# Order of sums and products at the seams of a two-layer kernel with Strassen products

## The chip, the cores and the metric

The kernel runs on one core of a Trainium2 chip. The core has a matrix engine (TensorE, PE in the profile), three engines for elementwise work (VectorE or DVE, ScalarE or ACT, GpSimd or POOL), a queue engine for transfers (SyncE or SP), and 16 DMA engines between device memory (DRAM) and the on-chip memories SBUF and PSUM. Each engine runs its own list of instructions in order, and waits on semaphores where it needs what another made. The metric is device microseconds of one execution; the time of a kernel is the median of its runs.

## The reference

There are eight batches of 256 tokens with 1024 features, in float32. Two layers follow each other, each with a residual:

```
layer 0:  y   = x + x·W0ᵀ + b0 + c_b · (x·(2·mask_b − 1))     mask_b: 8 integer matrices of 1024 x 1024
layer 1:  out = y + y·W1ᵀ + b1 + 2 · (y·A_s)·B_s               A_s, B_s: adapters of rank 16, s = itok[b]
```

So layer 0 has one weight matrix per batch, and layer 1 has one for all, with a small adapter per batch.

## The kernel before

Everything is computed transposed: weights are the stationary operand, tokens the moving one.

**Layer 0.** For each batch an effective weight is built in 8 pieces of 128x1024. ScalarE turns the integer mask into (2c·mask − c) (L237), VectorE adds the piece of W0ᵀ (L245), to which the identity was added so that the residual is in the product. `load` (L173) issues the transfers of a piece on SP; `build` does the two steps. The constant `BY_HALF` (L19) gives the number of first pieces, of batch 0, that are loaded and built as two halves, so that the product can begin with half a piece. Batch 0 (`first_batch`, matmuls L303) takes the pieces as they come. Batches 1 and 2 (`first_layer`, L278) are plain products. Batches 3 to 7 (`SEVEN`, L20; `class Seven`) use the Winograd form of Strassen's algorithm: seven products of half size (matmuls L419, into the PSUM tiles X, Y and Z) from sums of weight blocks (s1 to s4, `weight_sum`, L356) and of token blocks (t1 to t4, `token_sum`, L373). `Seven.operands` (L375) is a generator that gives these builds and sums in order; `Sevens.begin` (L500) makes some of them early, during other work, and `Sevens.run_one` keeps ten steps ahead of the products. Operands after the first `FREE_OPERANDS` (L491) of a group are ordered behind the end of the second layer of the group before. Results are read by ScalarE (`with_bias`, L438) and VectorE (`add`, L445).

**Layer 1.** `second_layer` (L694) is run for two groups of four batches, group 0 after batch 3 and group 1 after batch 7. Four batches are treated as a matrix of blocks, and Strassen's form is used twice: seven outer products named A11, A12, S1, S2, S4, S3, A22 (runs 0 to 6), each of them made of seven inner ones in X, Y and Z (`product`, L711, matmuls L718, four per inner product, two passes each in float32). The weight sums, the leaves, are made by VectorE during layer 0, stored to DRAM by POOL (`keep`, L533), and loaded by SP (`load_leaves`, L703, L708). Sums of y for an outer operand are made by `outer_sum` (L874, the T tiles) and its four inner sums by `Right.sums` (L685 to L691). The S3 weights are made again from reloaded blocks: `again` (L615) loads the tiles A11 and A21, L607 subtracts, `inner_in_place` (L596) makes the sums in place.

`run` (L785) is one outer product. Its accumulator X goes on being added to: it is read (`read`: a ScalarE copy, L772, where nothing is to be added, else a VectorE add, L774), then the next product is added into the same bank, and the following read takes the difference into account. So a product into X waits for the read before it. In run 0, `down` (L748) makes the adapters' first product: 64 matmuls passes into psh (L753), then four ScalarE activations into h_sb (L762). `up` (L727) makes the second, into banks G (L736), copied by ScalarE (L746). Quarters of the output are combined on VectorE (`add`, L860) and stored by POOL for group 0 (L781).

**What sets the order.** Instructions are recorded in the order of the text, but a scheduler may place them otherwise where it estimates that an operand is late. `behind(what)` (L144) fixes that an instruction is placed after the latest one remembered under that name. `ordered` (L891) does this for the sums of y. Generators given to `run` as `beside` are advanced by one step at fixed places, and emptied at the end of the run.

At the start `idle` (L98) issues matmuls on a zero tile, so that TensorE is busy while the first transfers come; h_sb, zeroed by VectorE (L95), serves as that tile and later holds the adapters' first product.

Of the kernel before, what the change touches and what calls it, by code (L numbers as in the profile page):

```python
# [9 lines left out]
F32 = mybir.dt.float32  # L10
# [4 lines left out]
P = 128  # L15
OH = 512
CG = 2
OQ = 256
BY_HALF = 3  # L19
SEVEN = (3, 4, 5, 6, 7)  # L20
SCALING = 2.0

# [2 lines left out]
def kernel(  # L25
# [38 lines left out]
    nc = tc.nc  # L64
    B, NG, _, _, T = xT.shape
# [25 lines left out]
    one_row = const.tile([1, P], F32, tag="one_row", name="one_row")  # L91
    nc.vector.memset(one_row, 1.0)

    h_sb = const.tile([P, T], F32, tag="h", name="h_sb")
    nc.vector.memset(h_sb, 0.0)  # L95
    idle_ps = psum.tile([P, T], F32, tag="ps", name="idle_ps")

    def idle(n: int):  # L98
        for _ in range(n):
            nc.tensor.matmul(idle_ps, lhsT=h_sb[:, :P], rhs=h_sb, start=True, stop=True)  # L100

    idle(1)
    c_ps = psum.tile([P, B], F32, tag="ps", name="c_ps")
    spread = nc.tensor.matmul(c_ps, lhsT=one_row, rhs=c_row, start=True, stop=True)
    with tc.issue_after(spread.ins):
# [38 lines left out]
    def behind(what: str):  # L144
        return tc.issue_after(anchors[what].ins) if what in anchors else nullcontext()
# [183 lines left out]
    class Seven:  # L329
# [45 lines left out]
        def operands(self):  # L375

            add, sub = nc.vector.tensor_add, nc.vector.tensor_sub
            for j in range(2):
                for a in range(2):
                    self.block(0, j, a)  # L380
                    yield
            self.token_sum("t1")
            yield
            self.token_sum("t2")
            yield
            for a in range(2):
                self.block(1, 1, a)
                yield
                self.block(1, 0, a)
                yield  # L390
                self.weight_sum("s1", add, "a21", "a22", a)
                yield
                self.weight_sum("s2", sub, "s1", "a11", a)
                yield
            self.token_sum("t3")
            yield
            for a in range(2):
                self.weight_sum("s3", sub, "a11", "a21", a)
                yield
            for a in range(2):  # L400
                self.weight_sum("s4", sub, "a12", "s2", a)
                yield
            self.token_sum("t4")
            yield
# [39 lines left out]
        def add(self, i, v, ps):  # L444
            anchors["weights"] = nc.vector.tensor_add(self.out(i, v), ps, self.out(i, v))  # L445
            if i == v:
                anchors["adds"] = anchors["weights"]
# [39 lines left out]
        HALVES = 14  # L487

    OPERANDS_AHEAD = 10
    FREE_OPERANDS = 7  # L490

    class Sevens:

# [12 lines left out]
        def run(self, y, between):  # L506

            for i, batch in enumerate(self.batches):
                batch.y = y[batch.b % GB]
                between(batch.b)  # L510
                self.run_one(i, batch)
# [182 lines left out]
    def second_layer(group: int, y, first, first_steps, second):  # L694
# [3 lines left out]
        a = la_of[group]  # L698
        halves = [[[y[2 * j + v][i] for v in range(2)] for j in range(2)] for i in range(2)]
        (b11, b12), (b21, b22) = halves  # L700
        left_leaf, right = {}, {}
# [9 lines left out]
        def product(ps, l, r, first=False, by_tile=False):  # L711
            order = [(c, j) for c in range(CG) for j in range(2)]
            if by_tile:
                order.sort(key=lambda cj: cj[1])

            with behind("products") if first else nullcontext(), behind("adapters"):
                for c, j in order:
                    anchors["inner"] = nc.tensor.matmul(  # L718
                        ps[:, j, :],
                        lhsT=l[:, c, j * P : (j + 1) * P],  # L720
                        rhs=r[:, c, :],
                        start=first and c == 0 and j == 0,
                        stop=False,
                        skip_group_check=True,
                    )
# [59 lines left out]
        def run(n, name, r, seed, out, dest=None, beside=None, early=None, mid=None, late=None, then=None):  # L785

            leaf = {k: left_leaf.pop((name, k)) for k in ("a11", "s1", "s2", "a12", "s3", "a22", "s4")}
            other = seed or {uv: None for uv in UV}  # L790
            beside = beside or iter(())
            X = banks.pop(n)

            def done(uv):
                if dest:
                    store(out[uv], *dest, *uv)
                if then:
                    then(uv)

            read(out[0, 0], X, other[0, 0])  # L800
            Z = bank(f"Z_{group}_{n}")
            product(Z, leaf["s1"], r.t["t1"], first=True)
            if early:
                early()
            product(X, leaf["s2"], r.t["t2"])
            next(beside, None)
            read(out[0, 1], X, other[0, 1])
            Y = bank(f"Y_{group}_{n}")
            product(Y, leaf["a12"], r.b[1, 0], first=True)
            read(out[0, 0], Y, out[0, 0])  # L810
            done((0, 0))
            if mid:
                mid()
            if n + 1 == len(plan):
                finish(X, Z, leaf, r, other, out, dest, beside, done)
                return
            product(X, leaf["s3"], r.t["t3"])
            next(beside, None)
            read(out[1, 1], X, other[1, 1])
            read(out[1, 1], Z, out[1, 1])  # L820
            done((1, 1))
            load_leaves(plan[n + 1])
            begin(n + 1, plan[n + 1], right[plan[n + 1]])
            next(beside, None)
            product(X, leaf["a22"], r.t["t4"])
            read(out[1, 0], X, other[1, 0])
            done((1, 0))
            next(beside, None)
            if late:
                late()  # L830
            product(Z, leaf["s4"], r.b[1, 1])
            read(out[0, 1], Z, out[0, 1])
            done((0, 1))
            for _ in beside:
                pass
# [19 lines left out]
        def quads(name):  # L855
            two = [pair(f"{name}{u}_{group}") for u in range(2)]
            return {(u, v): two[u][:, v] for u, v in UV}

        def add(o, x):
            nc.vector.tensor_add(o, o, x)  # L860
# [3 lines left out]
        big_t = {}  # L864

        def outer_sum(n, x, y, name):


            big_t[n] = [
                tpool.tile([P, TPH, T], F32, tag="T", name=f"T{n}_{group}_{v}") for v in range(2)  # L870
            ]
            right[name] = Right(f"T{n}_{group}", big_t[n])
            for v in range(2):
                nc.vector.tensor_sub(big_t[n][v], x[v], y[v])  # L874
                yield
            yield from right[name].sums()
# [7 lines left out]
        def next_weights(n):  # L884
            if group + 1 < NGROUP:
                while sevens[group + 1].made < n:
                    sevens[group + 1].begin(sevens[group + 1].made + 1)
                    yield


        def ordered(steps):  # L891

            while True:
                with behind("reads" if "reads" in own else "layer"):
                    if next(steps, True):
                        return
                yield

        own = {}
        s3 = ordered(later["S3"] if group == 0 else iter(()))  # L900
# [2 lines left out]
        begin(0, "A11", first)  # L903
        for _ in ordered(first_steps):
            pass
        t1 = ordered(outer_sum(1, b12, b11, "S1"))
        e1, c11, c12 = quads("e1"), quads("c11"), quads("c12")
        lower = (c11, c12)
        run(
            0, "A11", first, None, e1,  # L910
            beside=chain(islice(s3, 1), ordered(second.sums()), islice(s3, 4), islice(t1, 2)),
            early=down,
            mid=lambda: up(0, 0, lower),
            late=lambda: up(0, 1, lower),
            then=lambda uv: add(c11[0, 0], e1[0, 0]) if uv == (1, 1) else None,
        )
        for uv in UV[1:]:
            add(c11[uv], e1[uv])
        t2 = ordered(outer_sum(2, b22, big_t[1], "S2"))
        run(  # L920
            1, "A12", second, c11, c11,
# [16 lines left out]
        run(  # L938
            4, "S4", right["S4"], c12, c12,
            dest=(0, 1),  # L940
            beside=ordered(outer_sum(4, b21, big_t[2], "A22")),
            mid=lambda: up(1, 0, upper),
            late=lambda: up(1, 1, upper),
        )
# [1 line left out]
        def add_e5():  # L946

            for uv in UV:
                with behind("reads"):
                    add(c22[uv], e5[uv])  # L950
                yield

        run(5, "S3", right["S3"], e1, e1, beside=chain(add_e5(), next_weights(2)), then=lambda uv: add(c21[uv], e1[uv]))


        next_masks(6)
# [1 line left out]
        def last_quarter():  # L958
            for u, v in UV:
                add(c22[u, v], e1[u, v])  # L960
                store(c22[u, v], 1, 1, u, v)
                yield
# [1 line left out]
        run(  # L964
            6, "A22", right["A22"], c21, c21,
            dest=(1, 0),
            beside=chain(last_quarter(), next_weights(4)),
        )
        nonlocal limit
        limit = n_pieces  # L970


    load_to(LOADS_AHEAD)
# [141 lines left out]
```

## Time and profile before

| what | value |
|---|---|
| time, median of 3 runs | 412.66 us (411.93 to 412.89) |
| the profiled execution | 411.92 us |
| its span in the profile | 410.25 us (the page rounds to 410.3) |
| TensorE busy | 401.6 us, 98% of the span |
| VectorE busy | 312.2 us, 76% |
| ScalarE busy | 136.3 us, 33% |
| granted TensorE clock | 1.00 in every stage |
| layer 0, batches 0 to 2 | 5.7 to 90 us |
| batch 3 by seven products | 90 to 115 us |
| second layer, group 0 | 115 to 211 us |
| batches 4 to 7 by seven products | 211 to 313 us |
| second layer, group 1 | 313 to 407 us |

The span is what the profiler saw of the execution; the execution's time is 1.7 us longer. A line of the page or of the timeline names the engine, the line of the kernel, the operation, the tiles written and read, and in brackets how long the engine stood idle before it and what released it. In a line of the waits stand the engine, its line and tile, what it waited for, and then us in total, times, and the longest. A tile `T_t` stands for the four inner sums of a T tile, `b_t` for those of b11 or b21, `l_S_a<-leaf_S_a` for the load of a leaf.

### The profile page before, as it was taken

The page shows a single profiled execution, that of the slowest core. Times are in us where ns is not written, and L with a number is a line of the kernel's source. Part 1 is how long each engine was busy: PE and PEld are TensorE (multiplying, and loading weights), DVE is VectorE, ACT ScalarE, POOL GpSimd, SP SyncE. Part 2 cuts the span into 40 slices and gives each one's busy share as a digit, 9 for nine tenths or more (in the row PEclk, how much of TensorE's full clock was granted, in tenths as well). Part 3 has the DMA queues.
Part 4 walks back from the last instruction along what each step waited for, and adds up shares of the span by engine and source line. Part 5 has one row for each costly group of instructions (what it writes and reads, how often), then busy time and mean ns, then how long its engine had stood idle before and what let it go on. Part 6 is the DMA issues. An engine that isn't in the chain of part 4 may idle for free.

```text
span 410.3 us, 6785 instructions
## 1 busy us (share of the span) xinstructions
PE 401.6 (98%) x2554; PEld 358.1 (87%) x2554; DVE 312.2 (76%) x446; ACT 136.3 (33%) x221; POOL 52.0 (13%) x102
## 2 busy tenths in 40 slices
PE   8999999999999999999999999999999999999996
PEld 6788888899977887788899999999998788888885
DVE  2447696999834979885999999999922277898593
ACT  4444525782124203132140936538221420102200
POOL 0000152007850131011040000300000000000000
PEclk9999999999999999999999999999999999999999
DMA  7999999980898699676898848732022247655654
GB/s 277 403 403 397 400 410 419 403 321 16 302 350 312 214 309 330 194 254 210 286 378 312 309 162 279 260 95 79 27 63 75 80 129 237 171 153 165 214 154 153
DMA packets 41252, 99.56 MB, mean 243 GB/s; under 512 B 5636, under 2 KB 6148, under 8 KB 41220
## 3 DMA queue, kind: packets, MB, share of 16 engines
q1 hardware_dynamic: 32546, 76.04, 54.3%
q0 software_dynamic: 6224, 18.90, 12.3%
q10 hardware_dynamic: 2450, 4.20, 2.8%
q8 instruction: 20, 0.33, 0.3%
q14 instruction: 12, 0.10, 0.1%
HBM read 79.19 MB, written 19.92 MB: 242 GB/s over the span
## 4 chain that ended last, share of the span: by engine, by line
PE 90%; DMA 4%; DVE 3%; issue 1%; SPq 1%; ACT 0%; DVEq 0%
PE X L718 24%; PE X L419 17%; PE ps L278 13%; PE Z L718 11%; PE Z L419 8%; PE Y L718 5%; PE ps L303 4%; PE Y L419 3%; PE G L736 2%; PE psh L753 2%; DMA w_sb<-w0T 2%; DVE w L245 1%; DMA w<-mask 1%; DMA l_S_a<-leaf_S_a 1%; SPq L197 1%
## 5 line engine op out<-in xcount | busy, mean ns | idle before, releaser
L237 ACT ACTIVATE w<-w,neg_c,two_c 128x1024 f32<-128x1024 int32 (+1 forms) x67 | 78.5, 1207 | 64.1 <-DMA w<-mask 54.5
L245 DVE TENSOR_TENSOR w<-w,w_sb 128x1024 f32<-128x1024 f32 (+1 forms) x67 | 77.3, 1171 | 26.0 <-ACT w L237 16.1
L278 PE MATMUL ps<-x,w 128*128 128x256 f32 x256 | 55.4, 379 | 0.0
L278 PEld LDWEIGHTS ps<-x,w 128*128 128x128 f32 x256 | 48.6, 190 | 6.6
L438 ACT ACTIVATE y<-X,b_sb 128x128 f32<-128x128 f32 x60 | 17.1, 368 | 71.3 <-PE X L419 71.3
L860 DVE TENSOR_TENSOR c<-c,e 128x512 f32<-128x512 f32 x48 | 31.9, 682 | 4.6 <-ACT c L746 4.6
L419 PE MATMUL X<-t,s 128*128 128x128 f32 x288 | 34.0, 276 | 0.6 <-ACT y L438 0.3
L419 PEld LDWEIGHTS X<-t,s 128*128 128x128 f32 x288 | 33.0, 192 | 0.9 <-ACT y L438 0.5
L746 ACT COPY c<-G 128x512 f32<-128x512 f32 x32 | 16.4, 600 | 38.4 <-PE G L736 38.4
L303 PE MATMUL ps<-x,w 128*128 128x256 f32 x128 | 28.2, 381 | 0.9 <-DVE w L245 0.9
L303 PEld LDWEIGHTS ps<-x,w 128*128 128x128 f32 x128 | 24.2, 191 | 4.8 <-DVE w L245 1.5
L772 ACT COPY e<-X 128x512 f32<-128x512 f32 x16 | 9.4, 589 | 49.4 <-PE X L718 46.5
L774 DVE TENSOR_TENSOR e<-Y,e 128x512 f32<-128x512 f32 x8 | 5.5, 689 | 25.8 <-PE Y L718 14.0
L774 DVE TENSOR_TENSOR c<-X,c 128x512 f32<-128x512 f32 (+1 forms) x26 | 16.6, 645 | 8.1 <-PE X L718 7.9
L718 PE MATMUL X<-T_t,l_S_s 128*128 128x256 f32 x96 | 22.7, 379 | 0.0
L419 PE MATMUL X<-t,w 128*128 128x128 f32 x192 | 22.5, 276 | 0.0
L419 PEld LDWEIGHTS X<-t,w 128*128 128x128 f32 x192 | 21.9, 192 | 0.2 <-DVE y L445 0.2
L356 DVE TENSOR_TENSOR s<-w,w 128x1024 f32<-128x1024 f32 x18 | 21.7, 1217 | 0.1
L718 PEld LDWEIGHTS X<-T_t,l_S_s 128*128 128x128 f32 x96 | 18.2, 190 | 2.5
L419 PE MATMUL Z<-t,s 128*128 128x128 f32 x160 | 19.1, 275 | 0.3 <-DVE s L356 0.3
L419 PE MATMUL X<-x,w 128*128 128x128 f32 x160 | 18.8, 275 | 0.0
L419 PEld LDWEIGHTS Z<-t,s 128*128 128x128 f32 x160 | 18.4, 192 | 0.5 <-PE Y L419 0.5
(145 smaller groups left out, 670.7 us busy)
## 6 DMA issues: line engine op xcount, KB each, us to landing
w<-mask SPq DMA_DIRECT2D x61, 512.0 KB, 7.1
l_S_s<-leaf_S_s SPq DMA_DIRECT2D x32, 256.0 KB, 2.9
x<-xT SPq DMA_DIRECT2D x31, 256.0 KB, 7.4
l_A_s<-leaf_A_s SPq DMA_DIRECT2D x24, 256.0 KB, 2.8
l_S_a<-leaf_S_a SPq DMA_DIRECT2D x24, 256.0 KB, 2.8
w<-w1T SPq DMA_DIRECT2D x16, 256.0 KB, 6.9
outT<-c POOLq DMA_DIRECT2D x15, 256.0 KB, 4.6
outT<-c ACTq DMA_DIRECT2D x15, 256.0 KB, 2.5
```

The costliest lines, as they stand in the source:

```text
L237: nc.scalar.activation(w[:, i], m[:, i], AF.Identity, bias=neg_c[:, b : b + 1], scale=two_c[:, b : b + 1],)
L245: weff_at[k] = nc.vector.tensor_add(w[:, i], w[:, i], w0_of(k)[:, i])
L278: nc.tensor.matmul(ps[j // 2][:, j % 2, :], lhsT=w[:, c, j * P : (j + 1) * P], rhs=x_sb[b, g][:, c, :],  start=first and j % 2 == 0, stop= ...
L303: nc.tensor.matmul(ps[ot // 2][:, ot % 2, :], lhsT=w[:, h, j * P : (j + 1) * P], rhs=x_sb[0, c // CG][:, c % CG, :], start=c == 0 and ot % ...
L356: anchors["weights"] = op(s, self.w[x, a], self.w[y, a])
L419: anchors["products"] = nc.tensor.matmul(ps[:, j, :], lhsT=w[:, c, j * P : (j + 1) * P], rhs=r, start=first and a == 0 and c == 0 and j == ...
L438: sent = nc.scalar.activation(self.out(i, v)[:, j, :], ps[:, j, :], AF.Identity, bias=b0_sb[:, ot : ot + 1])
L718: anchors["inner"] = nc.tensor.matmul(ps[:, j, :], lhsT=l[:, c, j * P : (j + 1) * P], rhs=r[:, c, :], start=first and c == 0 and j == 0, s ...
L746: nc.scalar.copy(dest[b // 2][u, b % 2], ps[b])
L772: anchors["copies"] = nc.scalar.copy(out, ps)
L774: own["reads"] = anchors["reads"] = nc.vector.tensor_add(out, ps, other)
L860: nc.vector.tensor_add(o, o, x)
```

## The change

1. `BY_HALF` goes from 3 to 4: the fourth piece of batch 0, too, is loaded and built by halves.
2. The idle matmuls read a constant zero tile and not h_sb, so that h_sb isn't zeroed by VectorE at the start; two of them stand first and not one.
3. In `Seven.operands`, t1 and t2 come after the first two blocks of the lower row and not before them. This holds for batches 3 to 7.
4. `FREE_OPERANDS` goes from 7 to 6.
5. `product`: the first product into a bank was placed behind layer 0's last product alone; it is now placed behind the latest product of the second layer also. Together with the accumulation into one bank this puts TensorE's products in the order of the text.
6. `second_layer`: the first step of S3, the four sums of b21 (`second.sums`) and the two T1 tiles, which were advanced within run 0, are made ahead of run 0. The three adds into c11 after it are placed behind the latest read.
7. The weights of the next group's first batch: two pieces are built in run 4, two in run 5, two in run 6 (before: two in run 5, two in run 6), and the masks of eight pieces have been asked for at the end.

```
-BY_HALF = 3
+BY_HALF = 4
...
+    zeros = nc.const_aps.tensor(0.0, [P, T], F32)
     h_sb = const.tile([P, T], F32, tag="h", name="h_sb")
-    nc.vector.memset(h_sb, 0.0)
...
-            nc.tensor.matmul(idle_ps, lhsT=h_sb[:, :P], rhs=h_sb, start=True, stop=True)
-
-    idle(1)
+            nc.tensor.matmul(idle_ps, lhsT=zeros[:, :P], rhs=zeros, start=True, stop=True)
+
+    idle(2)
...
-            self.token_sum("t1")
-            yield
-            self.token_sum("t2")
-            yield
             for a in range(2):
                 self.block(1, 1, a)
                 yield
                 self.block(1, 0, a)
                 yield
+                if a == 0:
+                    self.token_sum("t1")
+                    yield
+                    self.token_sum("t2")
+                    yield
                 self.weight_sum("s1", add, "a21", "a22", a)
...
-    FREE_OPERANDS = 7
+    FREE_OPERANDS = 6
...
-            with behind("products") if first else nullcontext(), behind("adapters"):
+
+            with ExitStack() as place:
+                for what in ("products", "inner", "adapters") if first else ("adapters",):
+                    place.enter_context(behind(what))
                 for c, j in order:
...
         t1 = ordered(outer_sum(1, b12, b11, "S1"))
+        for _ in chain(islice(s3, 1), ordered(second.sums()), islice(t1, 2)):
+            pass
...
-            beside=chain(islice(s3, 1), ordered(second.sums()), islice(s3, 4), islice(t1, 2)),
+            beside=islice(s3, 4),
...
         for uv in UV[1:]:
-            add(c11[uv], e1[uv])
+            with behind("reads"):
+                add(c11[uv], e1[uv])
...
-            beside=ordered(outer_sum(4, b21, big_t[2], "A22")),
+            beside=chain(next_weights(2), ordered(outer_sum(4, b21, big_t[2], "A22"))),
...
-        run(5, "S3", right["S3"], e1, e1, beside=chain(add_e5(), next_weights(2)), then=lambda uv: add(c21[uv], e1[uv]))
+        run(5, "S3", right["S3"], e1, e1, beside=chain(add_e5(), next_weights(4)), then=lambda uv: add(c21[uv], e1[uv]))
...
-            beside=chain(last_quarter(), next_weights(4)),
+            beside=chain(last_quarter(), next_weights(6)),
...
+        next_masks(2 * NG)
```

## The prediction

> **What bounds the kernel now.** I read the page first, then the waits of TensorE, the table of stretches, and the timeline around every pause. Busy times and the chain that ended last, from the page:
>
> ```profile
> PE 401.6 (98%) x2554; PEld 358.1 (87%) x2554; DVE 312.2 (76%) x446; ACT 136.3 (33%) x221; POOL 52.0 (13%) x102
> ...
> PE 90%; DMA 4%; DVE 3%; issue 1%; SPq 1%; ACT 0%; DVEq 0%
> ```
>
> TensorE is the bound: 98% busy, 90% of the chain. The change removes no matmul, so it can only remove or add pauses of TensorE. These are the pauses (engine, line, what it waited for: us in all, times, longest):
>
> ```profile
> PE idle_ps L100 <- DVE h_sb L95: 1.4, 1, 1.4
> PE X L718 <- DMA l_S_a<-leaf_S_a: 1.4, 1, 1.4
> PE ps L303 <- DVE w L245: 0.9, 1, 0.9
> PE Z L718 <- issue: 0.4, 1, 0.4
> PE X L419 <- ACT y L438: 0.3, 1, 0.3
> PE Z L419 <- DVE s L356: 0.3, 1, 0.3
> PE X L419 <- DVE s L356: 0.2, 1, 0.2
> ```
>
> The records of busy matmuls hide part of a pause, so I measured each as the distance between starts of matmuls less the usual distance (0.216 us per 128x256 pass, 0.112 per 128x128). So measured, with about 0.10 us for refilling: 1.13 at 17.22 (fourth chunk), 0.8 at 142 to 146, 0.10 at 158, 1.63 at 165, 0.10 at 180, 0.52 at 218.6, 0.48 at 220.9, 0.60 at 226.8, 0.28 at 284.2. That is 5.6 us, all that a change of order can win after the start. Group 1's second layer (from 313) has no pause.
>
> Two more facts. Which engine fills the first 90 us besides (stretch, length, then PE, PEld, DVE, ACT, POOL busy; clock, DMA share, GB/s):
>
> ```profile
> 34.70:90.00 55.30, 55.30 (x259) 48.69 (x258) 46.18 (x67) 30.39 (x34) 10.39 (x19) 1.00 1.03 406
> ```
>
> The DMA engines are full (share 1.03), so nothing before 90 us can land earlier. And the timeline (start, length, engine, line) at the places that the change touches:
>
> ```profile
> 15.94 1.22 DVE L245 TENSOR_TENSOR w<-w,w_sb 128x1024 f32<-128x1024 f32 x1 [1.77 <-DMA w_sb<-w0T]
> 17.22 17.53 PE L303 MATMUL ps<-x,w 128*128 128x256 f32 x80 [0.87 <-DVE w L245]
> ...
> 86.06 5.14 ACT L237 ACTIVATE w<-w,neg_c,two_c 128x1024 f32<-128x1024 int32 x4 [0.73 <-DMA w<-mask]
> 86.51 0.76 DVE L373 TENSOR_TENSOR t<-x 128x256 f32<-128x256 f32 x2
> 87.18 0.75 DVE L373 TENSOR_TENSOR t<-x,t 128x256 f32<-128x256 f32 x2
> 87.85 2.35 DVE L245 TENSOR_TENSOR w<-w,w_sb 128x1024 f32<-128x1024 f32 x2
> 90.24 1.23 DVE L356 TENSOR_TENSOR s<-w,w 128x1024 f32<-128x1024 f32 x1
> ...
> 116.78 0.58 ACT L772 COPY e<-X 128x512 f32<-128x512 f32 x1 [0.59 <-PE X L718]
> 118.40 3.65 PE L753 MATMUL psh<-y,la 128*16 128x256 f32 x64
> 121.98 1.99 PE L718 MATMUL X<-b_t,l_A_s 128*128 128x256 f32 x8
> 122.20 1.57 ACT L762 ACTIVATE h_sb<-psh 16x256 f32<-16x256 f32 x4 [4.83 <-PE psh L753]
> ```
>
> [...]
>
> **The change part by part**, as a shift of TensorE against before, at matching instructions.
>
> Fourth chunk by halves. Before, its one 128x1024 add runs 15.94 to 17.16 and TensorE starts at 17.22. The w0 piece lands at 15.85. By halves, the first half lands earlier, and its activation (0.81) and add (0.69) are over at about 15.5; the second's at 16.8. TensorE ends the third chunk near 16.09, so it goes on at about 16.2 after a refill: a gain of 1.03. Two DMAs more at 0.33 us each on SP are hidden by the full DMA queue. But later landings stay: chunk 4 is built at 19.78 where TensorE now wants it at 19.65 (0.13 + 0.10), chunk 6 at 26.91 for 26.78 (0.13 + 0.10). L278 begins at 33.91 for 34.59: **−0.68**. Bounds: −1.1 (no new pauses) and −0.3 (halves delayed).
>
> Constant zeros, two idle matmuls. The 0.27 us memset ends and one 0.87 us pair more fills the wait for weights. The first real matmul at 5.41 waits for the w0 piece and its add at 4.66, the second half for the mask piece at 5.86. **0.** Without that cover −0.1 to +0.3; if the clock were not warm at 5.7, up to +1.7 (a cold pass takes 0.427, a warm one 0.216, eight passes).
>
> Batch 3's t1 and t2 two builds later. Four 128x256 passes of DVE, 1.34 us, ran at 86.51 to 87.85 in time in which DVE would else wait for ACT: the activations of the next two pieces end at 87.31 and 88.58, as their masks land, and cannot be earlier. Now DVE idles there and does the 1.34 us later. The first s1 starts at 91.09 for 90.24 (+0.85), and s2 of the second half ends at 99.32 for 98.47. TensorE wants it at 98.78 before, at 98.10 with the gain above. So it goes from −0.68 to 99.38 + 0.10 − 98.78 = +0.70: **+1.38**. Bounds 0 to 1.6; even without the delay of DVE 0.47 is lost, as the sum then stands at 98.47.
>
> Adapters and first read. In the built order of the changed program ScalarE's first read of X_0 (e<-X, L772) stands behind the four h_sb activations; before, it stood ahead (116.78 against 122.20). This holds for group 0 alone. TensorE's next matmuls add into the bank X_0 and so wait for that read. They began at 121.98; now psh must end, four activations run to 122.20 + 1.57 = 123.77, the copy takes 0.58, and the matmul begins at about 124.43: **+2.45**. A new wait, certain from the order; bounds 2.2 to 2.6.
>
> TensorE in the text's order. The pauses at 142 to 146 (0.8), 158 (0.1), 165 (1.63) and 180 (0.1) come from matmuls placed ahead of what they need; the sums of y (4 adds of 0.60) and T1 (2 of 1.17), now made before run 0, and the later place of X_4 remove them: X_4's leaf, issued near 162.4, lands 4.7 later (as at 160.28) at 167.1, and is wanted at 169.1. **−2.63.** Bounds −2.63 and 0.
>
> What stands behind the sums on DVE: the four S4 sums (L596) start at 118.75 instead of 113.29, their POOL stores go at 119.5 to 121.6, and the loads of A21, which wait for those, at about 124.5. They land by 131 (7.9 us at most before), then L607, and the reads of Y_0 and Z_0 end at 134.1. Z_0's second product wants its read at 136.2: hidden, 2.1 us to spare.
>
> Weights of batch 4. Two builds go into run 4, six weight pieces exist before batch 4. Its waits were
>
> ```profile
> 218.58 2.02 PE L419 MATMUL Z<-t,s 128*128 128x128 f32 x16 [0.29 <-DVE s L356]
> ...
> 220.85 2.02 PE L419 MATMUL X<-t,s 128*128 128x128 f32 x16 [0.25 <-DVE s L356]
> ...
> 226.78 3.84 PE L419 MATMUL X<-t,s 128*128 128x128 f32 x32 [0.34 <-ACT y L438]
> ```
>
> Two adds of 1.14 less in batch 4 make the sums ready at 217.8 for 218.65 and 221.9 for 222.0 (only 0.1 to spare): 0.52 + 0.48 + 0.60, **−1.60**; bounds −1.6 and −0.5. In runs 4 to 6 DVE is 44.08 us of 51 busy; the two builds fit, hidden by TensorE's products. One operand fewer ahead (L488) brings the y add before the builds at 284: **−0.28**, or 0.
>
> Sum: −0.68 + 1.38 + 2.45 − 2.63 − 1.60 − 0.28 = **−1.36 us**. The profiled execution took 411.92 (span 410.25); it becomes 410.56. The median of the runs is 412.66, 0.74 above; so 411.3.
>
> **Rivals.**
> - A, likeliest: the sum above, 411.3, by itself 410.6 to 412.0. 0.45.
> - B, batch 3 does not pause: landings there are earlier or the record's slack is larger. For: only 0.3 us of slack is a small margin of my walk. Against: ScalarE's waits for masks at 86.06. 411.3 − 1.38 = 409.9. 0.15.
> - C, the text's order does not remove the leaf's wait. A store issued at 154.90 took 7.7 us to land; a leaf as slow lands at 170.1, 1.0 late, plus refill: 412.4, no difference. Against: 4.7 is what that leaf took. 0.16.
> - D, slower: the A21 loads hold VectorE. Its queue is in order, and L607, waiting for them, stands ahead of the reads of Y_0 and Z_0. If they land at L after 133, all comes L − 133 later: it is slower than before from 134.4, by over 0.2% from 135.3; for L = 136, 414.3. For: those loads took 7.2 to 8.1 us, and start later now. Against: they were queued behind 14 stores, most of which are now over. 0.24, a part of which is for a new wait of this size that I have not found.
>
> **Numbers.** 0.2%, about what a measurement can tell from no change, is 0.83 us: faster means below 411.83, slower above 413.49. A lies below for nine tenths: 0.41 + B 0.15 = 0.56; the rest of A and C are 0.20 within; D 0.24. Range 409.8 to 414.0: it leaves out the lower end of B and the upper of D.
>
> **What would show it.** Right: matmuls of chunk k3 from 16.2; a pause of about 1.3 at the last s2 of batch 3 near 98; a pause of 2.45 before X_0's second product with the four h_sb activations ahead of the copy; no wait for l_S_a; no waits for s and y in batch 4. Wrong: no pause behind psh, a wait for e<-Z or for Y_0's bank near 133 to 138, or a lower clock after one.

## The result, and the profile after

The changed kernel took 411.89 us, the median of 14 runs (410.73 to 412.97); the kernel before, timed beside it, 412.11 us (14 runs). The ratio is 0.9988, interval 0.9972 to 1.0004: no difference that can be measured. The forecast was 411.3, a gain of 1.36 us; the median moved by 0.22, and the mean by 0.5 (411.76 for 412.25). The fourteen runs fall into two groups of seven, 410.73 to 411.58 and 412.20 to 412.97, which the third experiment takes up. The profiled execution took 411.16 us, and is of the lower group.

The page after, busy times and the chain that ended last:

```profile
PE 401.8 (98%) x2556; PEld 359.9 (88%) x2556; DVE 312.5 (76%) x446; ACT 136.9 (33%) x222; POOL 52.1 (13%) x102
...
PE 53%; issue 23%; DVE 10%; DMA 7%; POOL 6%; ACT 0%; SPq 0%; POOLq 0%; DVEq 0%
```

TensorE is as busy as before. The chain looks quite different, and should not be taken for a new bound: it walks back from releaser to releaser, and in this program the walk leaves TensorE at places where TensorE had no pause. The waits of TensorE say what changed (engine, line, what it waited for: us in all, times, longest):

```profile
PE X L722 <- ACT e L776: 2.4, 1, 2.4
PE idle_ps L100 <- PEq L1113: 0.9, 1, 0.9
PE X L420 <- DVE s L356: 0.7, 1, 0.7
PE X L420 <- DVE y L446: 0.2, 1, 0.2
```

Every wait of before is gone but the first at the start: no leaf, no w of the fourth chunk, no s or y of batch 4. Three new ones stand in their place. The stretch of batches 1 and 2, with the columns as before, is nearly unchanged, DMA engines still full (share 1.03):

```profile
34.70:90.00 55.30, 55.30 (x259) 48.69 (x258) 45.33 (x63) 30.63 (x34) 10.43 (x19) 1.00 1.03 405
```

The timeline after (start, length, engine, line) at the places where the forecast's steps are:

```profile
6.12 28.61 PE L303 MATMUL ps<-x,w 128*128 128x256 f32 x128
16.55 0.69 DVE L245 TENSOR_TENSOR w<-w,w_sb 128x512 f32<-128x512 f32 x1 [0.67 <-ACT w L237]
...
86.33 5.17 ACT L237 ACTIVATE w<-w,neg_c,two_c 128x1024 f32<-128x1024 int32 x4 [0.71 <-DMA w<-mask]
87.61 2.50 DVE L245 TENSOR_TENSOR w<-w,w_sb 128x1024 f32<-128x1024 f32 x2 [0.72 <-ACT w L237]
90.03 0.75 DVE L373 TENSOR_TENSOR t<-x 128x256 f32<-128x256 f32 x2
90.70 0.75 DVE L373 TENSOR_TENSOR t<-x,t 128x256 f32<-128x256 f32 x2
91.37 1.22 DVE L356 TENSOR_TENSOR s<-w,w 128x1024 f32<-128x1024 f32 x1
98.37 1.22 DVE L356 TENSOR_TENSOR s<-s,w 128x1024 f32<-128x1024 f32 x1
99.65 2.05 PE L420 MATMUL X<-t,s 128*128 128x128 f32 x16 [0.74 <-DVE s L356]
...
119.38 3.65 PE L757 MATMUL psh<-y,la 128*16 128x256 f32 x64
123.18 1.56 ACT L766 ACTIVATE h_sb<-psh 16x256 f32<-16x256 f32 x4 [6.00 <-PE psh L757]
124.76 0.59 ACT L776 COPY e<-X 128x512 f32<-128x512 f32 x1
125.40 1.99 PE L722 MATMUL X<-b_t,l_A_s 128*128 128x256 f32 x8 [2.38 <-ACT e L776]
...
258.59 3.62 PE L420 MATMUL X<-t,w 128*128 128x128 f32 x30 [0.15 <-DVE y L446]
```

Batch 0 now runs through without a pause. In batch 3 VectorE waits at 87.61 for ScalarE, does t1 and t2 at 90.03, and s2's second half comes at 99.6. Before, it came at 98.47:

```profile
97.25 1.22 DVE L356 TENSOR_TENSOR s<-s,w 128x1024 f32<-128x1024 f32 x1
```

The first read of X_0 (124.76) stands behind the four activations. A small pause appears in batch 5, at 258.6.

Measured as in the forecast, by distances between starts of matmuls, TensorE stands against before: −0.03 at the first matmul of L278 (34.56 for 34.59), +0.98 at the second layer (115.83 for 114.85), +0.77 at batch 4 (211.75 for 210.98), and −0.64 at the last matmul (405.55 for 406.19). The expectations below give three of these times for the changed kernel some 0.15 late: 34.7, 116.0, and 406.1, which is besides not where the last matmul begins but where its record ends (405.93 in the trace).

### The profile page after: what moved, and what is told of

It is laid out like the page before. It is cut to its first block, busy times and chain, and to the rows that moved or that the text cites. A ratio compares the mean times of both kernels' runs of the same rounds, so it can differ in the third digit from the quotient of the medians.

```text
span 409.5 us, 6788 instructions
## 1 busy us (share of the span) xinstructions
PE 401.8 (98%) x2556; PEld 359.9 (88%) x2556; DVE 312.5 (76%) x446; ACT 136.9 (33%) x222; POOL 52.1 (13%) x102
## 4 chain that ended last, share of the span: by engine, by line
PE 53%; issue 23%; DVE 10%; DMA 7%; POOL 6%; ACT 0%; SPq 0%; POOLq 0%; DVEq 0%
PE X L722 12%; PE ps L278 8%; PE X L420 8%; PE ps L303 7%; PE Z L722 6%; DVE s L356 4%; PE Z L420 3%; DVE w L245 3%; PE Y L722 3%; DMA x<-xT 2%; DMA w<-mask 2%; POOL outT L785 2%; DMA outT<-c 2%; PE Y L420 2%; DVE t L373 1%
## 5 line engine op out<-in xcount | busy, mean ns | idle before, releaser
L278 PE MATMUL ps<-x,w 128*128 128x256 f32 x256 | 55.4, 379 | 0.0
L278 PEld LDWEIGHTS ps<-x,w 128*128 128x128 f32 x256 | 48.6, 190 | 6.6
L303 PEld LDWEIGHTS ps<-x,w 128*128 128x128 f32 x128 | 25.1, 196 | 3.7
L778 DVE TENSOR_TENSOR c<-X,c 128x512 f32<-128x512 f32 (+1 forms) x26 | 16.7, 647 | 10.8 <-PE X L722 10.7
L420 PE MATMUL Y<-x,w 128*128 128x128 f32 x160 | 18.7, 275 | 0.0
L420 PEld LDWEIGHTS X<-x,w 128*128 128x128 f32 x160 | 18.4, 192 | 0.1
```

What stands on the lines that cost most here:

```text
L278: nc.tensor.matmul(ps[j // 2][:, j % 2, :], lhsT=w[:, c, j * P : (j + 1) * P], rhs=x_sb[b, g][:, c, :],  start=first and j % 2 == 0, stop= ...
L303: nc.tensor.matmul(ps[ot // 2][:, ot % 2, :], lhsT=w[:, h, j * P : (j + 1) * P], rhs=x_sb[0, c // CG][:, c % CG, :], start=c == 0 and ot % ...
L420: anchors["products"] = nc.tensor.matmul(ps[:, j, :], lhsT=w[:, c, j * P : (j + 1) * P], rhs=r, start=first and a == 0 and c == 0 and j == ...
L778: own["reads"] = anchors["reads"] = nc.vector.tensor_add(out, ps, other)
```

## The experiments

All ratios are to the kernel before, run on the same chip beside each kernel.

**The read of X_0 ahead of h_sb** (a_read). Edit to the changed kernel:

```
-                nc.scalar.mul(h_sb[rows, :], ph[rows, 0, :], SCALING)
+                with behind("copies"):
+                    nc.scalar.mul(h_sb[rows, :], ph[rows, 0, :], SCALING)
```

> The changed kernel with one edit: the four h_sb activations of the adapters are fixed behind ScalarE's first read of X_0. Theory (a wait of ScalarE's order): the pause of 2.45 us before X_0's second product goes, and nothing takes its place, since the read of Z_0 ends at 133.5 in the changed kernel and would be wanted at 134.1: TensorE's last matmul begins 2.45 us earlier, near 403.6 for 406.1; the time falls by about 2.4 us. Rival (the next thing late takes over, the A21 loads and the sums of y on VectorE): a new pause near 134 to 137, and less than 1.5 us gained.

409.22 us (408.95 to 409.87), ratio 0.9940 (0.9927 to 0.9952): 2.7 us below the changed kernel's median, more than the pause. In the trace the pause of 2.45 is gone, and another has come (timeline of this kernel):

```profile
131.75 0.69 DVE L608 TENSOR_TENSOR A<-A,A 128x512 f32<-128x512 f32 x1 [10.00 <-DMA A<-w1T]
132.36 0.68 DVE L779 TENSOR_TENSOR e<-Y,e 128x512 f32<-128x512 f32 x1
...
134.16 0.68 DVE L779 TENSOR_TENSOR e<-Z,e 128x512 f32<-128x512 f32 x1
...
134.90 1.99 PE L722 MATMUL Z<-y,l_A_s 128*128 128x256 f32 x8 [0.65 <-DVE e L779]
```

VectorE waits for the A21 loads, the reads of Y_0 and Z_0 stand behind, and TensorE waits for Z_0's: 0.71, with 0.10 for the refill (the first matmul pass behind a pause stands 0.32 us ahead of the second, at 17.22 before and at 125.40 in the changed kernel, the following ones 0.22 apart). So both expectations held in part: the profiled execution gained 1.69 us at the last matmul (it begins at 403.86 for 405.55) and not 2.45, as the rival said that something late would be next. The load that VectorE waits for was issued as in the changed kernel (124.80 for 124.86), but landed at 131.72 for 130.26; had this load and the next landed as there, the read of Z_0 would have ended near 133.5, in time, as the theory said. Why it landed later is open. And the median gained 2.7. The trace of one execution doesn't explain that; the third and fifth experiments do.

**t1 and t2 back** (a_t12: the four yields of `token_sum("t1")` and `("t2")` ahead of the lower blocks again).

> The changed kernel with t1 and t2 of all batches by seven products back ahead of the lower blocks. Theory (VectorE waits for masks where it did t1 and t2 before, and does them later): s2's second half is ready about 0.9 us earlier and the pause of 1.00 us at 98.8 goes or falls under 0.2; TensorE's first matmul of the second layer stands at 115.0 for 116.0, and about 1.0 us is gained at the end. Rival (the pause comes from masks that land later in the changed kernel): the pause stays within 0.3 us of 1.0.

410.23 us (409.53 to 412.50, 17 runs), ratio 0.9969 (0.9957 to 0.9980). The second layer's first matmul starts at 115.07, as expected, 0.76 us earlier than in the changed kernel. A pause stays in batch 3, 0.43 and 0.10 for the refill (0.90 and 0.10 in the changed kernel), as TensorE comes there 0.28 us earlier in this run. The delay by t1 and t2 is shown, and its size: from the start of ScalarE's activation at 86.3 (the first of the four in its line above, which begins as its mask lands) to the end of s2's second half it takes 13.25 or 13.26 us in the four profiles with the late place, and 12.41 to 12.43 in the eight with the early one, so 0.84. The masks' landing counts beside it: that activation begins at 86.06 before, at 86.33 in the changed kernel, at 86.43 here, and anywhere from 85.44 to 86.50 over the twelve profiles.

**The old start** (a_idle: h_sb zeroed and read by the idle matmuls, `idle(1)`).

> The changed kernel with the start of the kernel before: h_sb zeroed by VectorE, idle matmuls on h_sb, one ahead and not two. Theory (the matmul too many and the late clock cost 0.8 us at the start, but the pause in batch 3 takes it in, because the masks set the end of s2 there): the first matmul of L278 stands about 0.7 us earlier (33.9 for 34.7), the pause at 98.8 grows from 1.0 to 1.5 or more, and the end moves by less than 0.4 us. Rival (the 0.8 us arrive at the end): the last matmul begins 0.8 us earlier. Second rival (the late clock is a matter of the run, not of the zero tile): the first matmul of L278 stands where it stood.

411.82 us (410.52 to 412.87, 22 runs), ratio 0.9992 (0.9980 to 1.0004): nothing. L278 begins at 34.29 for 34.56, but in the two kernels above, which have the changed start, at 34.26 and 34.28: the second rival holds. How long the first matmuls run at half speed is a matter of the execution: in the kernel before the passes begin 0.43 us apart up to 5.41 and 0.22 from 5.72, in the changed kernel 0.43 up to 7.40 and 0.22 from 7.80; and the last six idle passes take 2.93 us in the changed kernel and 2.60 in the kernel of the fifth experiment, both with the changed start, 2.77 before and 2.93 here with the old one. And the pause of batch 3 grew to 1.20 and 0.10, as the theory said, though by less: what TensorE gains before 98 us it waits there, and the second layer begins at 115.85 for 115.83.

The profile of this run showed something else. It took 412.87 us, the top of its range, and this is the timeline after the pause, then the stretch around it (length; busy PE, PEld, DVE, ACT, POOL; granted clock, DMA share, GB/s):

```profile
125.42 3.68 PE L722 MATMUL X<-b_t,l_A_s 128*128 128x256 f32 x8 [2.38 <-ACT e L776]
```

```profile
125.20:129.00 3.80, 3.58 (x9) 2.86 (x10) 0.00 (x0) 0.17 (x1) 1.84 (x4) 0.55 0.95 290
```

Eight passes take 3.68 us where the changed kernel's profile shows 1.99, and the granted clock of the stretch is 0.55. The profile of the kernel with t1 and t2 back, of an execution of 412.09 us, shows the same, 3.43 us, and a granted clock of 0.55 from 124.70 to 128.40. So the pause can cost the clock as well, 1.7 us more by the starts of the matmuls behind it in both profiles. The two groups of the changed kernel's runs are this: the mean granted clock on record is 0.999 or 1.000 for each of the lower seven and 0.994 or 0.996 for each of the upper seven. Here it is at most 0.996 in eleven of the 22 runs, all of 411.85 or more, and in the kernel with t1 and t2 back in five of 17, all of 411.33 or more. The changed kernel's profiled execution was of the lower group, and shows no loss of clock.

**All three edits** (a_three).

> All three edits together on the changed kernel: the first read of X_0 ahead of h_sb, t1 and t2 back, the old start. Theory: 2.45 from the read; of the 1.0 of batch 3 and the 0.8 of the start together 1.0 to 1.4, as s2's second half is ready near 98.5 to 98.7 and TensorE comes near 98.0. The last matmul begins 3.4 to 3.9 us earlier (402.2 to 402.7 for 406.1), time about 408.3. Rival (additive): 4.24 us, 401.8.

407.98 us (407.03 to 408.44), ratio 0.9905 (0.9891 to 0.9919). The last matmul begins at 402.44 in the trace for 405.55 in the changed kernel's: 3.11 us earlier, a little under the theory's 3.4 to 3.9, and the gains don't add up to 4.24. Its pause before Z_0's last product is 0.29 and 0.10, that of batch 3 0.22 and 0.10.

**The pause filled** (a_fill). Edit to the changed kernel, in `down` for group 0:

```
+                spare = bank("fill")
+                for _ in range(5):
+                    with behind("adapters"):
+                        anchors["adapters"] = nc.tensor.matmul(
+                            spare[:, 0, :], lhsT=zeros[:, :P], rhs=zeros, start=True, stop=True
+                        )
```

> The changed kernel with five matmuls on the zero tile into a spare bank between the adapters' first product and X_0's second product: they take 2.16 us of the pause of 2.45 and end before the read of X_0 that sets its end, so the pause of useful work stays as long. Theory (the times of the changed kernel fall into two groups, near 410.9 and near 412.4, because after the pause the clock of TensorE falls in some executions: the two profiles with the pause and a time over 412 show eight matmuls at half speed after it): with TensorE busy through the pause there is one group, spread under 1.2 us, near 410.9, and no matmul after the pause at half speed. Rival (two groups for another reason, such as the start): both groups stay, with a gap near 412.

410.58 us (410.30 to 411.33), ratio 0.9967 (0.9954 to 0.9980). One group, where the changed kernel had two, and the lower one. The timeline: the useless matmuls take the place of the pause, and X_0's second product takes 1.99 us as in an undisturbed execution.

```profile
122.06 2.44 PE L768 MATMUL fill<-const-float32-0.0 128*128 128x256 f32 x10
122.28 1.56 ACT L773 ACTIVATE h_sb<-psh 16x256 f32<-16x256 f32 x4 [6.00 <-PE psh L757]
124.50 1.99 PE L722 MATMUL X<-b_t,l_A_s 128*128 128x256 f32 x8
```

Work that computes nothing gained 1.3 us of the median, and 1.0 of the mean. VectorE's read of Y_0 came one place earlier in this build, which no wait of TensorE shows; so it is the pause's effect on the clock that went. By five runs alone one group could be luck, with seven of fourteen in each; but the mean clock is 0.999 or 1.000 in all five, and the profiles with the clock at 0.55 and the clocks of the two groups point the same way.

**TensorE in the text's order alone**, on the kernel before (b_text: the edit to `product` only).

> The kernel before with TensorE in the text's order alone. ScalarE keeps the first read of X_0 ahead of the four h_sb activations there. Theory: the pauses at 142 to 146, 158, 165 and 180 go without the sums being made earlier, as their operands are then wanted 1.7 to 3.5 us later; no pause of 2.45 us; last matmul 2.4 to 2.7 us earlier than in the kernel before. Rival (the early sums are what makes the text's order possible): pauses of over 1 us remain between 135 and 150.

413.60 us (412.24 to 414.85, 13 runs), ratio 1.0032 (1.0018 to 1.0047): slower. The theory fell. The pauses at 142 to 180 are gone, but one of 2.85 us has come (timeline):

```profile
137.45 1.89 DVE L607 TENSOR_TENSOR A<-A,A 128x512 f32<-128x512 f32 x3
139.26 2.35 DVE L876 TENSOR_TENSOR T<-y,y 128x1024 f32<-128x1024 f32 x2
...
142.74 0.68 DVE L776 TENSOR_TENSOR c<-X,c 128x512 f32<-128x512 f32 x1
...
143.47 2.72 PE L720 MATMUL X<-b_t,l_A_s 128*128 128x256 f32 x8 [2.69 <-DVE c L776]
```

X_1's second product comes earlier in the text's order, and VectorE's read of X_1 stands behind the S3 subtractions and T1. Here the order of TensorE needs the early sums: they are one change in two places. The early sums without the order were not run. The clock fell after this pause too (eight passes in 2.72 us for 1.99, a mean clock of 0.996 in the profile), and in six of the 13 runs the mean clock is 0.996 or less; the other seven have a median of 412.62.

**The weights' moving alone**, on the kernel before (b_weights: `next_weights` in runs 4 to 6, and the masks at the end).

> The kernel before with the weights of batch 4 over runs 4 to 6 alone (two pieces, four, six, and the masks asked for at the end); seven operands free as before. Theory: the three pauses of batch 4 (1.6 us) go; no pause of over 0.2 us at 258 in batch 5 if that one comes from one operand fewer ahead, and the one at 284 stays: 1.4 to 1.6 us gained. Rival: the pause in batch 5 (0.42) comes from the weights' moving, it shows here, and 1.2 us are gained.

410.84 us (409.54 to 413.13, 9 runs), ratio 0.9963 (0.9949 to 0.9978). Batch 4's pauses are gone, but for 0.07 and 0.09 us, and the one at 284 with them. The pause in batch 5 is there, 0.21 and 0.10, though seven operands are free: the rival holds, it comes from the moving. Both together are 0.31 or 0.32 in every profile with the weights moved and t1 and t2 in their old place, with six or with seven operands free, and 0.42 where t1 and t2 are late: so 0.1 of the changed kernel's pause goes with their place. The median gained 1.4 us; by the trace it is 1.4 in batch 4 and 0.28 at 284 less 0.31 in batch 5. In the profiled execution, of 413.13 us, the leaf of X_4 came 1.0 us later than in the kernel before, and the clock fell after that pause of 2.58 us (eight passes in 2.79 us for 1.89, a mean clock of 0.996 in the profile); in the eight other runs the mean clock is 1.000.

**T1 within run 0 again** (best1), on the kernel with three edits:

```
-        for _ in chain(islice(s3, 1), ordered(second.sums()), islice(t1, 2)):
+        for _ in chain(islice(s3, 1), ordered(second.sums())):
...
-            beside=islice(s3, 4),
+            beside=chain(islice(s3, 4), islice(t1, 2)),
```

> The changed kernel with the first read of X_0 ahead of h_sb, t1 and t2 back, the old start, and the two T1 tiles within run 0 again (the sums of b21 stay ahead). Theory: the pause of 0.29 + 0.10 us before Z_0's last product, which the same kernel with T1 ahead of run 0 showed, is VectorE's read of Z_0 behind the S3 subtraction that waits for the A21 loads, late because 2.4 us of T1 stand ahead of the S4 sums: it goes, and 0.3 to 0.4 us with it; time near 407.6. Rival: T1 made later makes the first product of run 2 or its sums late, a new pause near 138 to 142 and no gain or a loss.

408.69 us (408.31 to 408.93), ratio 0.9913 (0.9901 to 0.9926): no better than with T1 ahead: 0.7 above by the medians, though the intervals of the two ratios overlap. Z_0's pause is gone, and X_1's second product waits 1.04 us for VectorE's reads (a wait of "PE X L721 <- DVE c L778"). The rival holds.

**The S3 subtractions out of run 0**, on the kernel with three edits (best4: run 0 without `islice(s3, 4)`, run 1 with `chain(t1, islice(t2, 2), islice(s3, 4))`, run 2 with `chain(t2, s3, ...)`).

> The kernel with all three edits, and the S3 subtractions out of run 0: they go behind the T2 tiles of run 1, the S3 sums into run 2. T1 stays ahead of run 0. Theory: in run 0 nothing stands ahead of VectorE's reads of Y_0 and Z_0 that waits for the A21 loads, and the pause of 0.29 + 0.10 us before Z_0's last product goes; the subtractions are hidden in run 2, whose leaves are wanted only in run 5: 0.3 to 0.4 us gained, time near 407.6. Rival: VectorE is too full in runs 1 to 4 for them, and a new pause of T2's or T3's sums between 150 and 175 takes the gain.

410.03 us (409.58 to 411.71, 18 runs), ratio 0.9966 (0.9955 to 0.9977): worse by 2. Z_0's pause is gone, and a pause of 2.12 us stands at 166.5, where X_3's second product waits for its read behind the S3 sums (timeline):

```profile
165.76 0.68 DVE L778 TENSOR_TENSOR e<-X,e 128x512 f32<-128x512 f32 x1
...
166.50 1.99 PE L721 MATMUL X<-T_t,l_S_s 128*128 128x256 f32 x8 [1.96 <-DVE e L778]
```

Its runs fall into groups again, eleven from 409.58 to 410.07 and seven from 411.00 to 411.71. No profile of an execution of the upper one was taken, but its seven runs have a mean clock of 0.994 to 0.996, and the eleven others 0.998 to 1.000: the clock fell there too, and that it fell after this pause is argued.

**The fourth chunk whole**, on the kernel with three edits (half3: `BY_HALF = 3`).

> The kernel with all three edits (first read of X_0 ahead of h_sb, t1 and t2 back, the old start), and the fourth chunk whole again. Theory: the fourth chunk costs a pause of 0.8 to 1.1 us near 16 to 17, TensorE comes to batch 3 some 0.4 to 0.7 us later, and the pause of 0.3 us at s2's second half takes that much in: 0.1 to 0.4 us lost at the end, time 408.1 to 408.4. Rival (nothing absorbs it): 0.7 to 1.1 us lost, 408.7 or more.

408.14 us (407.63 to 408.97), ratio 0.9909 (0.9895 to 0.9923), for 407.98 with halves: 0.16, no difference that these runs can tell. In the trace the chunk's pause is back, 1.01 and 0.10 us, L278 begins at 34.62 for 34.28 (the kernel with halves had a pause of 0.79 at 8.3 that this one lacks), and the second layer at 114.89 for 114.86: batch 3 took in 0.31 of 0.34, and so its pause is gone. The last matmul begins 0.65 later than with halves, and that is the pause before Z_0's last product, 0.91 for 0.29. It isn't the chunk's: the A21 load that the second S3 subtraction waits for was issued at 124.21 for 124.17 and landed at 132.15 for 131.50. Halves are worth 0.3 us in batch 0 in these two profiles, and next to nothing at the second layer.

## Why the prediction was right or wrong

The measured time lies in the range, and on the side of no difference, to which 0.20 had been given; a gain beyond 0.2% had 0.56. The range of 4.2 us reaches from a clear gain to a clear loss, so that to lie in it says little; the steps say more. As shifts of TensorE in the profiled executions:

| step | predicted | measured |
|---|---|---|
| start: halves, zeros, idle | −0.68 | −0.03 |
| batch 3, t1 and t2 | +1.38 | +1.00 |
| read of X_0 behind h_sb | +2.45 | +2.45 |
| text's order, early sums | −2.63 | −2.65 |
| batch 4 | −1.60 | −1.55 |
| batch 5 | 0 | +0.42 |
| batch 6 | −0.28 | −0.28 |
| sum | −1.36 | −0.64 |

- **The read of X_0** was right in its mechanism and to the hundredth, from the order of ScalarE's instructions and four durations. The trace shows that order. The product that the copy reads was done before psh's began at 119.38, and the copy still starts at 124.76, behind the activations of 123.18 that wait for psh; with the order edited (a_read) it starts at 117.70. VectorE did the same in a_read: its reads of Y_0 and Z_0 came at 132.36 and 134.16, behind the subtraction of 131.75 that had waited 10.00 us for a load.
- **What failed there** is that the forecast charged the pause with its own length alone. In two of three profiles of kernels that had it unfilled, this pause of 2.45 us cost the clock as well, 1.7 us each. In the changed kernel it costs 2.45 us by its length, and about 1.5 more in half of the executions, by the medians of the two groups (410.96 and 412.41). The forecast had put that cost at nothing, and its list has no rival on it, though it names a lower clock among the signs of being wrong. It is most of why the gain was small: the seven runs that kept the clock have a median 1.15 us below the kernel before, near the forecast's 1.36, and with the other seven the gain is 0.22 by the medians and 0.5 by the means.
- **Text's order and sums**: right, and b_text shows that the gain is not the order's alone.
- **D**, the A21 loads: those that the first subtraction needs landed by 130.3 in the changed kernel, and the read of Z_0 ended at 133.5; no wait. The rival was wrong there and right one step later: with the pause of 2.45 taken away, and loads that landed 1.5 later, it is the next thing late (0.71).
- **C and B** did not come: no wait for a leaf, and batch 3 paused.
- **Batch 3**: the mechanism was right. The delay by t1 and t2 was forecast as 0.85 and measured as 0.84; s2's second half was ready at 99.59 for 99.32 as worked out, since the masks landed 0.27 later. The step is smaller than forecast because TensorE came 0.65 later than forecast and so waited less. The forecast took the landings of one execution as fixed; over the profiles they vary by 1.1 us. Its own logic says what else follows, and I didn't draw it: as masks fix the end of s2, all that is won before 98 us is waited for there. a_fill came to L278 at 33.59, 1.0 earlier than the kernel before, and to the second layer at 114.93, 0.08 later.
- **The start**: "0" for the zeros holds (a_idle), −0.68 for the halves was missed in the one profile, since the passes came to full speed only at 7.80 us. The bound for a cold clock, +1.7, was there; in this profile the first four of the eight passes took 0.40 to 0.43 us each and the other four 0.22, and the idle matmuls ended 0.40 later. Over the eight profiles with halves L278 begins 0.03 to 0.99 us earlier than the kernel before's 34.59. That batch 3 lost less than forecast, 1.00 for 1.38, made up for a part of this.
- **Batch 4**: right. **Batch 5**: I had said that no stall comes. With the weights ahead, the scheduler places batch 6's t1 to t3 before the builds at 254, and the y add stands behind three builds until 257.85. b_weights lays 0.31 of the 0.42 to the moving; the rest is found only where t1 and t2 are late.

Open: why a load that is issued at the same time lands up to 1.5 us later in one execution than in another, and what decides in which executions a pause of this length costs the clock.

## What to carry to other kernels

Read the built order of every engine, not TensorE's alone: here one copy, moved by a scheduler behind four activations that wait for TensorE, undid a gain of 2.65 us, and a single ordering line won it back with more (ratio 0.9940, with two edits more 0.9905). Work gained ahead of a point that transfers fix was lost at that point (a_fill, 1.0 us ahead of the kernel before at L278 and 0.08 behind it at the second layer). And where a kernel's runs fall into two groups, look at the granted clock of each run and profile one of the upper group: here a pause of 2.45 us was paid twice in seven of fourteen executions, once as a pause and once in the clock.

## What was not expected of the hardware

Behind the pause of TensorE of 2.45 us, in front of X_0's second product, the granted clock was 0.55 over the following 3.7 to 3.8 us in two profiles (a_idle from 125.20 to 129.00, a_t12 from 124.70 to 128.40). In the changed kernel's profile, behind the same pause, it was 1.00 (columns as before):

```profile
125.40:128.80 3.40, 3.40 (x16) 2.96 (x16) 0.00 (x0) 0.59 (x1) 1.62 (x4) 1.00 1.00 302
```

In front of the pause TensorE had run the adapters' product, 64 passes with 16 columns in 3.65 us. Pauses of 2.58 (b_weights) and 2.85 us (b_text), behind full-width products, lowered the clock as well: to a mean of 0.996 over each of the two profiles, with eight passes in 2.79 us for 1.89 and in 2.72 for 1.99. With five matmuls on zeros in the pause (a_fill) the mean clock was 0.999 or 1.000 in all five runs. Why the clock fell behind the same pause in seven of the changed kernel's fourteen runs and stayed in the other seven is not shown.
